# A two-layer recurrent kernel: TensorE's order in the second layer written out by hand, and half of a group's inverse moved into the next step

## The chip, the cores and the metric

The kernel runs on one core of a Trainium2 chip, as one launch. The metric is the device time of an execution in microseconds (us), lower being better. A core has five engines that run their own instruction streams in order and meet at semaphores: TensorE (PE: matmuls and transposes into PSUM; PEld is its weight load), VectorE (DVE), ScalarE (ACT), GpSimd (POOL), and SyncE (SP), which issues DMAs; POOL issues DMAs too.

## The reference

One sequence of 1024 tokens with 256 channels runs through two layers. Each layer normalises, computes an attention branch `s` and a mixture-of-experts branch `g` from the same normalised input, and adds `s * silu(g)`. The change is in the second layer. Its attention branch is a gated delta rule with 32 value heads and 16 key heads of 128 channels, behind a causal convolution of four taps; its expert branch picks 2 of 8 experts per token.

```python
    def step(S, xs):                       # per head, over the tokens
        qt, kt, vt, gt, bt = xs
        S = S * jnp.exp(gt)[..., None, None]
        kS = jnp.einsum('bhk,bhkv->bhv', kt, S)
        S = S + bt[..., None, None] * kt[..., :, None] * (vt - kS)[..., None, :]
        o = jnp.einsum('bhk,bhkv->bhv', qt, S)
        return (S, o)
    ...
    mixed = hidden_states @ W_qkv
    z = (hidden_states @ W_z).reshape(B, T, NV, DV)
    beta = jax.nn.sigmoid(hidden_states @ W_b)
    g = -jnp.exp(A_log) * jax.nn.softplus(hidden_states @ W_a + dt_bias)
    mixed = _silu(conv(mixed, conv_w))
    q, k, v = jnp.split(mixed, [key_dim, 2 * key_dim], axis=-1)
    q = _l2norm(q) * DK ** (-0.5)
    k = _l2norm(k)
    o = _gated_delta_rule(q, k, v, g, beta)
    o = o * jax.lax.rsqrt(mean(o * o) + 1e-06) * norm_w * _silu(z)
    return o.reshape(B, T, value_dim) @ W_out
    ...
x = x + s * g                              # g = silu(experts(xn))
```

## The kernel before

**The tiling.** The second layer works in `NG` = 8 groups of two key heads and four value heads. Time is cut into `NT` = 8 chunks of 128 tokens. Inside a chunk the delta rule is solved as matrices: a 128x128 triangular matrix per head and chunk (tile `m`) is inverted, and the state `S` is carried from chunk to chunk. Projections are done with a high and a low part of each operand, three matmuls of 128x512 for a product (`mm3`, L69 to L71).

**The streams.** Work is written as generators (streams), one letter each, and a string says in which order items are emitted:

- K, Q, V (`proj_k`, `proj_q`, `proj_v`): load weights (`load_w`, with `split_weights`: a DMA on SP's queue, one on POOL's, and a subtraction on POOL, L49), project into PSUM tile `pc`, and convolve (`conv_tile`: one ACT instruction and three DVE instructions of 128x511 for each half of 512 tokens, L678 and L681).
- P (`pre`): for each chunk the decay (`decay`: a POOL selection into `b`, L729, a matmul into `pe`, L731, an exponential into `d`), the scores of k with itself (`pkk`, L751) and the matrix `m` (L762). After the chunks comes the solve: POOL copies the 32x32 diagonal blocks into `Ad`, and 31 pairs of DVE instructions (L791, L793) with transposes around them (L785 to L800) give `X`, then `Un` and `Ut`. Then the inverse is completed on PE from 32x32 blocks (L818 to L827) and 64x64 blocks (L838, L843), in two halves of 16 matrices, each with POOL copies of `Ut` into `m` in front (L811).
- R (`recs`, `rec`): the recurrence, one item per chunk. `pkq` (L855) is the scores of q; then for both key heads `j`: four transposes into `pt` (L865), which ACT copies to `kd` and `bv`; `pk` (L883, L887), the state applied to k and q; DVE adds the first to `bv` (L885); `pw` (L893), the inverse applied to `bv`; ACT copies it to `W` (L895); `ps` (L900), whose result DVE adds to `S` (L909); and `pmw` (L915), which DVE adds to `v` (L918).
- O (`outp`, `out_half`): projection of z into `pz`, the gate in `gz` (L964 to L971, with transposes into `pto`, L970), a split into `yh` and `yl` (L973, on POOL), projection `pout` (L979 to L982), copies into `st`, and a DMA that adds to `sTd` in HBM (L988).
- F (`ffn_blocks`): blocks of 128 tokens of the experts, 12 at the start and 11 in the last step: transposes `pxt` (L1017), `pg` (L1024), transposes `pht` (L1033), `pd` (L1039), a store.
- U: the SiLU of what the convolutions left.

**What sets the order.** The scheduler orders all engines' instructions of the second layer from estimated times, dependencies and priorities. The strings `START`, `STEP` (for each group) and `LAST` (last group) only say in which order the items are emitted; P has a priority 3000 ahead, K one 1000 behind, and within `rec` the parts behind `pk` have 1000. `STEP` contains for one group the items of R of that group, O of the group before, and K, P, V, Q of the next. Instructions of the first layer already stand in an order written by hand (L519).

**PSUM.** Eight banks: ring C of three (`pc`, `pz`, `pto`, `pout` and F's), ring R of three (`pkq`, `pt`, `pk`, `pw`, `ps`, `pmw`) and ring B of two (`pe`, `pkk` and the inverse's `pm`, `pm2`, `pm3`). A tile takes the next bank of its ring, and its first matmul waits until the readers of the tile before in that bank are done.

**Before and behind the groups.** In front of `START` 16 indirect DMAs of POOL (`moe.scatter`, L215) put the tokens in the order of the experts. Behind the last group 16 indirect gathers (`moe.gather`, L222, into `yg`) bring the experts' results back, the sums in `sTd` are read into `sT`, transposed (`pfs`, L1190) and combined (L1191 to L1194).

```python
START = 'UPPPPPPPPPPPPVVVVQQUPPPPKKFFFFFFFFFFFFU'
STEP = 'OPPPPRPROPOPRPRVRPVOURPVRPRPPKKQPPRPQVU'
LAST = 'RROORRFFROOFFRFFRFFRFFR'
```

Of the kernel before, what the change touches and what calls it, by code (L numbers as in the profile page):

```python
# [8 lines left out]
F32 = mybir.dt.float32  # L9
# [15 lines left out]
def f32(ap):  # L25
    return ap.bitcast(F32)
# [93 lines left out]
class Blocks:  # L120
# [91 lines left out]
    def scatter(self, tc, t, x):  # L212

        for k in range(self.K):
            ins = self.nc.gpsimd.indirect_dma_start(out=self.xs[:, :], out_offset=bass.IndirectOffsetOnAxis(ap=self.to[:, t, k : k + 1], axis=0),  # L215
                                                    in_=x, in_offset=None).ins
            for other in self.scatters:
                tc.declare_no_dep(ins, other, reason="different rows")
            self.scatters.append(ins)

# [347 lines left out]
ZT = True  # L568
PBUFS = {'C': 3, 'R': 3, 'B': 2}
PS = {'pc': 'C', 'pxt': 'C', 'pg': 'C', 'pht': 'C', 'pe': 'B', 'pkk': 'B', 'pm': 'B', 'pm2': 'B', 'pm3': 'B', 'pkq': 'R', 'pt': 'R', 'pk': 'R', 'pw': 'R', 'ps': 'R', 'pmw': 'R', 'pz': 'C', 'pto': 'C', 'pout': 'C', 'pd': 'C', 'pfs': 'R'}  # L570
OLAG = 4
PRIO = {'P': 3000, 'U': 200, 'K': -1000}
AB = 'DVE'
RC = (0, 1000, 1000)
WINDOWS = True
FSEG = (12, 11)
NB = {'k0': 4, 'k1': 4, 'q0': 2, 'q1': 3, 'v': 8, 'm': 4, 'b': 3, 'd': 13, 'yh': 1, 'yl': 1, 'gz': 2, 'w': 3, 'S': 3, 'kd': 4, 'bv': 3, 'W': 1, 'bt': 1, 'tmp': 1, 'wr': 1, 'st': 1, 'ct': 1}
OR, KD, SP = 'Pool', 'ACT', True
GPRIO = 2000
EARLY = 'KK'  # L580
START = 'UPPPPPPPPPPPPVVVVQQUPPPPKKFFFFFFFFFFFFU'
STEP = 'OPPPPRPROPOPRPVRVPOURPVRPRPPKKQPPRPQVU'
LAST = 'RROORRFFROOFFRFFRFFRFFR'


def l1_block(ctx, tc, c, x1, wqkv, wz, wb, wa, convw, dtb, alog, normw, wout, wr, wg, wu, wd, out, x1_done=lambda: None):
# [27 lines left out]
    if ZT:  # L614
        nc.vector.tensor_scalar(nw, nw, 0.5, None, ALU.mult)
# [24 lines left out]
    silus = []  # L640

    def do_silus():
        while silus:
            d = silus.pop(0)
            table("silu", nc.scalar.activation(d, d, AF.Silu))

    def table(kind, ins):

        if not WINDOWS:
            return  # L650
        if kind != win[0]:
            win[0], win[1], win[2] = kind, win[2], []
        for before in win[1]:
            tc.add_manual_dep(ins.ins, before.name, mybir.DependencyInfo(mybir.DependencyClass.NoSync, mybir.DependencyReason.DATA),
                              reason="table sets")
        win[2].append(ins.ins)
# [11 lines left out]
    def conv_tile(w, j, n, dst):  # L668

        for h, d in enumerate(dst):  # L670
            p = ps("pc", [128, 512])
            project(p, w, j, slice(512 * h, 512 * h + 512))
            if h:

                nc.scalar.activation(d[:, 3:512], p[:, 3:512], AF.Copy, scale=cw[:, n, 3:4])
                nc.vector.scalar_tensor_tensor(d[:, 0:3], p[:, 0:3], cw[:, n, 3:4], last, ALU.mult, ALU.add)
            else:
                nc.scalar.activation(d, p, AF.Copy, scale=cw[:, n, 3:4])  # L678
            for i in (2, 1, 0):
                o = 3 - i  # L680
                nc.vector.scalar_tensor_tensor(d[:, o:512], p[:, 0 : 512 - o], cw[:, n, i : i + 1], d[:, o:512], ALU.mult, ALU.add)  # L681
            if not h:

                last = tiny.tile([128, 3], F32, tag="last", name="last")
                nc.vector.tensor_scalar(last, p[:, 509:512], cw[:, n, 0:1], None, ALU.mult)
                for i in (1, 2):
                    nc.vector.scalar_tensor_tensor(last[:, 0 : 3 - i], p[:, 509 + i : 512], cw[:, n, i : i + 1], last[:, 0 : 3 - i], ALU.mult, ALU.add)  # L687
        silus.extend(dst)
        if not WINDOWS:
            do_silus()  # L690
# [4 lines left out]
    def halves(pool, tag, b0, b1):  # L695
        return [pool.tile([128, 512], F32, tag=tag + str(h), name=tag, bufs=b) for h, b in enumerate((b0, b1))]

    def proj_k(g, G):

        G.k = []  # L700
        w = load_w(wqkv, slice(2048 + 256 * g, 2048 + 256 * g + 256))
        for j in range(2):
            G.k.append(halves(kp, "k", NB["k0"], NB["k1"]))
            conv_tile(w, j, 16 + 2 * g + j, G.k[j])
            yield
    def proj_q(g, G):
        G.q = []
        w = load_w(wqkv, slice(256 * g, 256 * g + 256))
        for j in range(2):
            G.q.append(halves(qp, "q", NB["q0"], NB["q1"]))  # L710
            conv_tile(w, j, 2 * g + j, G.q[j])
            yield

    def proj_v(g, G):

        G.v = []
        for j in range(2):
            w = load_w(wqkv, slice(4096 + 512 * g + 256 * j, 4096 + 512 * g + 256 * j + 256))
            G.v.append([vp.tile([128, 2, 512], F32, tag="v", name="v") for _ in range(2)])
            for i in range(2):  # L720
                conv_tile(w, i, 32 + 4 * g + 2 * j + i, [v[:, i, :] for v in G.v[j]])
                yield

    def decay(g, cc):

        p = ps("pe", [128, 512])
        for i in range(2):
            b = rc.tile([128, 4, 128], FR, tag="b", name="b", bufs=NB["b"])
            nc.gpsimd.affine_select(b, f32(gs)[:, cc, g, i, :, None].to_broadcast([128, 4, 128]), [[0, 4], [1, 128]], ALU.is_ge, 0.0,  # L729
                                    base=0, channel_multiplier=-1)  # L730
# [5 lines left out]
    def pre(g, G):  # L736
# [7 lines left out]
        rk = rc.tile([128, NT, 2], F32, tag="rk", name="rk")  # L744
        for cc in range(NT):
# [14 lines left out]
            if AB == "DVE":  # L760
                for u in range(4):
                    nc.vector.scalar_tensor_tensor(m4[:, u], p[:, u // 2, :], cf[:, cc, u : u + 1], d[:, u, :], ALU.mult, ALU.mult)  # L762
            elif AB == "Pool":
                for u in range(4):
                    nc.scalar.activation(m4[:, u], p[:, u // 2, :], AF.Copy, scale=cf[:, cc, u : u + 1])
                nc.gpsimd.tensor_tensor(m4, m4, d, ALU.mult)
            else:
                nc.vector.tensor_tensor(m4.rearrange("p (a b) t -> p a b t", b=2), p[:, :, None, :].to_broadcast([128, 2, 2, 128]), d.rearrange("p (a b) t -> p a b t", b=2), ALU.mult)
                nc.gpsimd.tensor_tensor(m4, m4, cf[:, cc, :, None].to_broadcast([128, 4, 128]), ALU.mult)

            nc.gpsimd.affine_select(d, d, [[0, 4], [1, 128]], ALU.is_ge, 0.0, base=0, channel_multiplier=-1)
            yield
        rsqrt(nc, tiny, rk.rearrange("p a b -> p (a b)"), kss.rearrange("p a b -> p (a b)"), 2 * NT)
# [14 lines left out]
        for j in range(31):  # L788
# [5 lines left out]
            if j % 8 == 7:  # L794
                yield
# [6 lines left out]
        pool_copy(nc, Un[32:64, :, 32:64], Un[32:64, :, 0:32])  # L802
        yield

        P = bt.tile([128, 32, 32], F32, tag="b2", name="P")
        for h in range(2):
            us = slice(16 * h, 16 * h + 16)
            M = G.m[h]
            for i in range(4):
                s = slice(32 * i, 32 * i + 32)  # L810
                pool_copy(nc, M[s, :, s], Ut[s, us])  # L811
            nc.gpsimd.memset(M[32:64, :, 0:32], 0.0)
            nc.gpsimd.memset(M[96:128, :, 64:96], 0.0)
            nc.gpsimd.memset(M[64:128, :, 0:64], 0.0)
            p = ps("pm", [128, 16, 32])
            for u in range(16):
                uu = 16 * h + u
                nc.tensor.matmul(p[32:64, u, :], M[0:32, u, 32:64], Un[0:32, uu, 0:32], start=True, stop=True, tile_position=(0, 32))  # L818
                nc.tensor.matmul(p[96:128, u, :], M[64:96, u, 96:128], Un[64:96, uu, 0:32], start=True, stop=True, tile_position=(64, 96))
            nc.scalar.copy(P[32:64, us, :], p[32:64])  # L820
            nc.scalar.copy(P[96:128, us, :], p[96:128])
            p = ps("pm", [128, 16, 32])
            for u in range(16):
                uu = 16 * h + u
                nc.tensor.matmul(p[0:32, u, :], P[32:64, uu, :], Ut[32:64, uu, :], start=True, stop=True, tile_position=(32, 0))
                nc.tensor.matmul(p[32:64, u, :], Ut[32:64, uu, :], P[32:64, uu, :], start=True, stop=True, tile_position=(32, 32))
                nc.tensor.matmul(p[64:96, u, :], P[96:128, uu, :], Ut[96:128, uu, :], start=True, stop=True, tile_position=(96, 64))  # L827
            nc.scalar.copy(M[0:32, :, 32:64], p[0:32])
            nc.scalar.copy(Un[32:64, us, 0:32], p[32:64])
            nc.scalar.copy(M[64:96, :, 96:128], p[64:96])  # L830
            yield
            for q in range(2):
                qs = slice(8 * q, 8 * q + 8)
                p = ps("pm2", [128, 8, 64])
                P2 = P[64:128, us].rearrange("p (a b) c -> p a (b c)", b=2)
                for u in range(8):
                    uu = 8 * q + u
                    nc.tensor.matmul(p[64:128, u, :], M[0:64, uu, 64:128], Un[0:64, 16 * h + uu, :], start=True, stop=True, tile_position=(0, 64))  # L838
                nc.scalar.copy(P2, p[64:128])
                p = ps("pm3", [64, 8, 64])  # L840
                for u in range(8):
                    uu = 8 * q + u
# [401 lines left out]
```

## Time and profile before

| What | Value |
|---|---|
| Median of three executions | 1928.91 us (1925.61 to 1929.60) |
| The profiled execution | 1922.61 us, span 1920.6 us |
| Mean clock granted to TensorE in it | 0.918 |
| PE busy | 1581.3 us (82%), 11566 matmuls |
| DVE busy | 1339.8 us (70%) |
| ACT busy | 1053.3 us (55%) |
| POOL busy | 754.5 us (39%) |
| DMA | 147.28 MB, mean 77 GB/s |

The profile is one execution. "Busy" is the time in which an engine executes; the matmuls are pipelined, so their busy time is longer than the distance between two starts. Its second part cuts the span into 40 slices of 48 us, with a digit for the busy share in tenths. Costly groups of instructions are listed with the idle time of their engine in front of them and what released it:

```profile
L69 PE MATMUL pc<-xnh,wl 128*128 128x512 f32 x256 | 118.5, 464 | 42.1 <-DVE last L687 12.3
L893 PE MATMUL pw<-bv,m 128*128 128x128 f32 x512 | 92.4, 300 | 71.5 <-DVE bv L885 67.6
L681 DVE SCALAR_TENSOR_TENSOR v<-pc,cw,v 128x511 f32<-128x511 f32 (+2 forms) x192 | 140.3, 740 | 2.6 <-ACT v L678 1.7
L907 POOL TENSOR_TENSOR S<-S,eC 128x256 f32<-128x256 f32 x96 | 59.6, 621 | 182.9 <-PE pk L887 147.8
```

In the second line, for example, the 512 `pw` matmul passes were busy for 92.4 us at 300 ns each, and PE stood idle for 71.5 us in front of them, 67.6 of it until DVE had written `bv`.

### The profile page before, as it was taken

The page shows a single profiled execution, that of the slowest core. Times are in us where ns is not written, and L with a number is a line of the kernel's source. Part 1 is how long each engine was busy: PE and PEld are TensorE (multiplying, and loading weights), DVE is VectorE, ACT ScalarE, POOL GpSimd, SP SyncE. Part 2 cuts the span into 40 slices and gives each one's busy share as a digit, 9 for nine tenths or more (in the row PEclk, how much of TensorE's full clock was granted, in tenths as well). Part 3 has the DMA queues.
Part 4 walks back from the last instruction along what each step waited for, and adds up shares of the span by engine and source line. Part 5 has one row for each costly group of instructions (what it writes and reads, how often), then busy time and mean ns, then how long its engine had stood idle before and what let it go on. Part 6 is the DMA issues. An engine that isn't in the chain of part 4 may idle for free. (4 is left out here: it accounts for less than half of the span.)

```text
span 1920.6 us, 34083 instructions
## 1 busy us (share of the span) xinstructions
PE 1581.3 (82%) x11566; PEld 1207.1 (63%) x11566; DVE 1339.8 (70%) x3833; ACT 1053.3 (55%) x2844; POOL 754.5 (39%) x949
## 2 busy tenths in 40 slices
PE   4789988989656699889799799799799799879854
PEld 3446666666444377667677577677677677658643
DVE  6675565555659827947977978978978977963332
ACT  2345545544423356646677566576576566646632
POOL 4051000000616425157347347347347347433263
PEclk9799999999858679979999999999999999989977
DMA  8024444441362421012103203103103103204535
GB/s 261 12 86 129 127 120 126 131 133 60 104 147 78 116 69 52 17 35 61 39 24 67 44 24 72 39 24 72 39 24 72 39 23 72 63 16 98 139 88 124
DMA packets 149755, 147.28 MB, mean 77 GB/s; under 512 B 22013, under 2 KB 137037, under 8 KB 149581
## 3 DMA queue, kind: packets, MB, share of 16 engines
q1 hardware_dynamic: 115853, 97.15, 17.1%
q0 software_dynamic: 33728, 47.96, 11.9%
q8 instruction: 92, 1.51, 0.3%
q14 instruction: 82, 0.67, 0.1%
HBM read 91.59 MB, written 49.28 MB: 73 GB/s over the span
## 5 line engine op out<-in xcount | busy, mean ns | idle before, releaser
L493 ACT ACTIVATE pe<-p 128x1024 f32<-128x1024 f32 (+1 forms) x192 | 154.6, 813 | 113.6 <-PE p L491 83.5
L427 DVE CUSTOM_DVE_ANT_0 junk<-p,maskm 128x128 bf16<-128x128 f32 (+3 forms) x256 | 125.2, 489 | 59.7 <-PE p L421 48.9
L69 PE MATMUL pc<-xnh,wl 128*128 128x512 f32 x256 | 118.5, 464 | 42.1 <-DVE last L687 12.3
L893 PE MATMUL pw<-bv,m 128*128 128x128 f32 x512 | 92.4, 300 | 71.5 <-DVE bv L885 67.6
L681 DVE SCALAR_TENSOR_TENSOR v<-pc,cw,v 128x511 f32<-128x511 f32 (+2 forms) x192 | 140.3, 740 | 2.6 <-ACT v L678 1.7
L893 PEld LDWEIGHTS pw<-bv,m 128*128 128x128 f32 x512 | 74.8, 194 | 100.2 <-DVE bv L885 87.0
L421 PE MATMUL p<-kz,qT 128*128 128x512 f32 (+3 forms) x384 | 116.7, 396 | 19.7 <-DMA kz<-kT 11.5
L907 POOL TENSOR_TENSOR S<-S,eC 128x256 f32<-128x256 f32 x96 | 59.6, 621 | 182.9 <-PE pk L887 147.8
L487 PE MATMUL p<-q,kz 128*128 128x512 f32 (+3 forms) x384 | 122.6, 404 | 6.8 <-ACT pe L493 2.2
L923 ACT ACTIVATE sq<-v 128x128 bf16<-128x128 f32 x256 | 77.3, 307 | 88.8 <-DVE v L918 78.7
L49 POOL TENSOR_TENSOR wl<-wr,wh 128x512 fp32r<-128x512 f32 x68 | 88.4, 1301 | 94.5 <-DMA wh<-in_L_attn_W_z_dram 24.2
L895 ACT ACTIVATE W<-pw,cf 128x128 f32<-128x128 f32 x256 | 79.9, 365 | 60.0 <-PE pw L893 58.4
L965 DVE SCALAR_TENSOR_TENSOR gz<-gz,pz 128x512 f32<-128x512 f32 x64 | 43.8, 685 | 92.6 <-ACT gz L964 92.4
L71 PE MATMUL pc<-xnl,wh 128*128 128x512 f32 x256 | 107.4, 420 | 0.0
L70 PE MATMUL pc<-xnh,wh 128*128 128x512 f32 x256 | 107.2, 419 | 0.0
L874 ACT ACTIVATE kd<-pt,eR 128x128 f32<-128x128 f32 x256 | 79.8, 361 | 45.7 <-PE pt L865 44.3
L423 DVE TENSOR_REDUCE mx<-p 128x2 f32<-128x1024 f32 x64 | 77.8, 1223 | 32.7 <-PE p L421 32.1
L793 DVE TENSOR_TENSOR X<-X,Ad 128x31 f32<-128x31 f32 (+15 forms) x248 | 97.6, 394 | 3.8
L791 DVE TENSOR_TENSOR Ad<-Ab,X 128x31 f32<-128x31 f32 (+15 forms) x248 | 93.4, 376 | 3.3
L421 PEld LDWEIGHTS p<-kz,qT 128*128 128x128 f32 x384 | 66.1, 202 | 40.8 <-ACT pe L493 10.1
L973 POOL TENSOR_TENSOR yl<-gz,yh 128x512 fp32r<-128x512 f32 x64 | 84.0, 1315 | 19.3 <-ACT yh L972 19.1
L69 PEld LDWEIGHTS pc<-xnh,wl 128*128 128x128 f32 x256 | 51.9, 203 | 62.3 <-DVE last L687 12.8
(356 smaller groups left out, 5062.8 us busy)
## 6 DMA issues: line engine op xcount, KB each, us to landing
sTd<-st POOLq DMA_DIRECT2D x32, 512.0 KB, 6.4
gw<-_L_ffn_gate_up_proj_dram SPq DMA_DIRECT2D x64, 192.0 KB
l0xs<-zero SPq DMA_DIRECT2D x1, 8320.0 KB
xb<-l0xs SPq DMA_DIRECT2D x32, 256.0 KB
l0ys<-y SPq DMA_DIRECT2D x32, 256.0 KB
wh<-in_L_attn_W_qkv_dram POOLq DMA_DIRECT2D x32, 256.0 KB, 3.1
wr<-in_L_attn_W_qkv_dram SPq DMA_DIRECT2D x32, 256.0 KB
dw<-in_L_ffn_down_proj_dram SPq DMA_DIRECT2D x64, 96.0 KB
```

The costliest lines, as they stand in the source:

```text
L49: nc.gpsimd.tensor_tensor(lo, raw, f32(hi), ALU.subtract)
L69: nc.tensor.matmul(out, al, bh, start=start, stop=False)
L70: nc.tensor.matmul(out, ah, bh, start=False, stop=False)
L71: nc.tensor.matmul(out, ah, bl, start=False, stop=stop)
L421: nc.tensor.matmul(p[:, h - h0, :n], qT[:, 128 * i : 128 * i + 128], kz[:, h, 512 * j : 512 * j + n], start=True, stop=True)
L427: nc.vector.tensor_tensor_reduce(junk[:, :n], p[:, h - h0, :n], maskm[:, o : o + n], 1.0, -3e38, ALU.add, ALU.max, accum_out=mx[:, i, h, 0:1])
L487: nc.tensor.matmul(p[:, h - h0, :n], kz[:, h, 128 * kt : 128 * kt + 128], q2[:, 512 * qb + o : 512 * qb + 512], start=True, stop=not diag)
L493: nc.scalar.activation(e[:, :, :n], p[:, :, :n], AF.Exp, scale=SC)
L681: nc.vector.scalar_tensor_tensor(d[:, o:512], p[:, 0 : 512 - o], cw[:, n, i : i + 1], d[:, o:512], ALU.mult, ALU.add)
L791: nc.vector.tensor_tensor(t, Ab[:, j, j + 1 : 32, None].to_broadcast([128, n, m]), X[:, j, None, 0:m].to_broadcast([128, n, m]), ALU.mult)
L793: nc.vector.tensor_tensor(X[:, j + 1 : 32, 0:m], X[:, j + 1 : 32, 0:m], t, ALU.add)
L893: nc.tensor.matmul(pw[:, 0, i, :], M[:, 4 * (cc % 4) + 2 * j + i, :], bv[:, i, :], start=True, stop=True)
```

## The change

Nothing is computed differently. The streams are cut into smaller items, their emission is spread by position instead of by a string, and PE executes the second layer's instructions in the order of emission. The other engines are still ordered by the scheduler.

- `weave` takes entries (stream, number of items, from, to), spreads that many items evenly between two positions in the step, sorts, and emits. `START`, `STEP` and `LAST` are lists of such entries; all runs within `tc.manual_schedule` for PE.
- `rec` becomes five kinds of items: `scores` (`pkq`), `turn` (transposes), `state` (`pk` and the add to `bv`), `delta` (`pw`, and the copy, now in place into `bv`), and `update` (`ps`, `S`, `pmw`, squares). Per chunk both `j` are interleaved, 9 items, and `scores` and `turn` of the next chunk come early. The recurrence has 72 items a group instead of 8. `ps` uses the second half of the bank of `pw`. `bv` has 4 buffers instead of 3; `W` is gone.
- P is split into P (decay and scores, 8 items), X (the solve, 32 items) and I (inverse, 12 items). In `STEP` six items of I (a half, for chunks 0 to 3) come late in the step in which X was solved, and the other six (chunks 4 to 7) early in the next step.
- K, Q and V give one item per half tile. The last half of Q of a group is projected in the next step (`late_q`), with its weights loaded a second time.
- O: a half is cut in two items for `pz` and `gz`, two for `pto` and `yh`, `yl`, and two for `pout`; `pout` of one half (`pend`) comes after `pz` of the next. Weights are loaded one item ahead.
- F: a block is cut into `turn_x`, `up`, `turn_h` and `down`, and the blocks overlap: `turn_h` and `down` of a block come between `turn_x` and `up` of the next. Its work tile is an `m` buffer of its own instead of `gz`, `yh` and `yl`. All 12 first blocks are in `START`, ahead of the recurrence of group 0; the last two blocks of the other 11 come at the end of `LAST`.
- The scatters are emitted within `START` and ordered on POOL behind the last decay selection emitted before them.

```diff
-START = 'UPPPPPPPPPPPPVVVVQQUPPPPKKFFFFFFFFFFFFU'
-STEP = 'OPPPPRPROPOPRPRVRPVOURPVRPRPPKKQPPRPQVU'
-LAST = 'RROORRFFROOFFRFFRFFRFFR'
+START = (("P", 8, 0, 0.3), ("S", 8, 0.3, 0.31), ("V", 9, 0, 0.45), ("Q", 5, 0.15, 0.5), ("U", 1, 0.52, 0.52), ("X", 32, 0.3, 0.6), ("I", 6, 0.7, 1),
+         ("F", 52, 0.35, 1), ("K", 1, 0.9, 0.9))
+STEP = (("R", 72, 0, 1), ("K", 5, 0, 0.08), ("U", 1, 0.09, 0.09), ("O", 24, 0, 0.45), ("P", 8, 0.09, 0.38), ("X", 32, 0.37, 0.5),
+        ("V", 1, 0.27, 0.27), ("V", 4, 0.36, 0.58), ("Q", 1, 0.45, 0.45), ("V", 4, 0.62, 0.82), ("Q", 3, 0.52, 0.7), ("U", 1, 0.85, 0.85),
+        ("I", 6, 0.02, 0.36), ("I", 6, 0.66, 0.9), ("K", 1, 0.92, 0.92), ("O", 1, 0.93, 0.93))
+LAST = (("R", 72, 0, 1), ("I", 6, 0.02, 0.36), ("K", 1, 0, 0.1), ("U", 1, 0.12, 0.12), ("O", 24, 0, 0.45), ("O", 1, 0.5, 0.5), ("O", 12, 0.55, 1),
+        ("F", 48, 0.3, 1.2), ("O", 12, 1, 1.4))
...
+    def late_q(g, G):
+        if G.q[1][1] is None:
+            w = load_w(wqkv, slice(256 * g, 256 * g + 256))
+            G.q[1][1] = half(qp, "q", 1)
+            conv_half(w, 1, 2 * g + 1, 1, G.q[1][1])
...
+        def delta(cc, j):
+            kd, bv = st[cc, j]
+            pw = st[cc, j, 0] = ps("pw", [128, 2, 2, 128])
+            for i in range(2):
+                nc.tensor.matmul(pw[:, 0, i, :], G.m[cc // 4][:, 4 * (cc % 4) + 2 * j + i, :], bv[:, i, :], start=True, stop=True)
+            with tc.high_priority(offset=RPRIO):
                 for i in range(2):
+                    nc.scalar.activation(bv[:, i, :], pw[:, 0, i, :], AF.Copy, scale=G.cf[:, cc, 2 * j + i : 2 * j + i + 1])
+
+        def update(cc, j):
...
+            kd, W = st.pop((cc, j))
+            pS = st.pop((cc, j, 0))[:, 1]
...
+        scores(0)
+        yield
+        turn(0, 0)
+        yield
+        turn(0, 1)
+        yield
+        for cc in range(NT):
+            more = cc + 1 < NT
+            for j in range(2):
+                state(cc, j)
+                yield
+            if more:
+                scores(cc + 1)
+                yield
+            for j in range(2):
+                delta(cc, j)
+                yield
+            if more:
+                turn(cc + 1, 0)
+                yield
+            for j in range(2):
+                update(cc, j)
+                yield
+            if more:
+                turn(cc + 1, 1)
+                yield
...
+    def weave(*lists):
+        items = []
+        for s, n, a, b in lists:
+            items += [(a + (b - a) * (i + 0.5) / n, s) for i in range(n)]
+        for _, s in sorted(items, key=lambda x: x[0]):
+            next(streams[s], None)
...
-    for t in range(NT):
-        xt = rc.tile([128, D], F32, tag="kd", name="xt", bufs=NB["kd"])
-        nc.sync.dma_start(xt, xnd[128 * t : 128 * t + 128, :])
-        moe.scatter(tc, t, xt)
-    run(START)
-    for g in range(NG):
-        run(LAST if g == NG - 1 else STEP if g else STEP.replace("O", "", OLAG))
-    run("FFFF" + "".join(s * 16 for s in "PROF"))
+    def scatters():
+        for t in range(NT):
+            xt = rc.tile([128, D], F32, tag="kd", name="xt", bufs=NB["kd"])
+            nc.sync.dma_start(xt, xnd[128 * t : 128 * t + 128, :])
+            for ins in moe.scatter(tc, t, xt):
+                order_only(ins, last_b[0].ins)
+            yield
+
+    streams["S"] = scatters()
+    with tc.manual_schedule(engines={mybir.EngineType.PE}):
+        weave(*START)
+        for g in range(NG):
+            weave(*(LAST if g == NG - 1 else [x for x in STEP if g or x[0] != "O" or x[1] == 1]))
```

## The prediction

> **What bounds the kernel now.** I read the slices of the whole span first, then windows of one step of the second layer, then the waits in that step, and the chain that ended last. The first layer (to about 530 us) is not touched.
>
> ```profile
> PE   4789988989656699889799799799799799879854
> DVE  6675565555659827947977978978978977963332
> PEclk9799999999858679979999999999999999989977
> ```
>
> From slice 17 on the pattern 7-9-9 for PE repeats every three slices of 48 us: one step is 144 us. The last `pmw` matmul (L915) of groups 0 to 7 stands at 812, 981, 1118, 1263, 1406, 1550, 1698 and 1837 us in the trace, so six steps (812 to 1698) take 886, 147.7 each, and the last group 139. The slices at clock 5 to 7 (520 to 720 us) are the start of the layer; those behind 1837 are its tail of 83 us.
>
> ```profile
> 672.00:720.00 48.00, 45.55 (x563) 35.97 (x562) 14.23 (x39) 24.90 (x66) 11.35 (x18) 0.72 0.24 69
> 1296.00:1344.00 48.00, 43.95 (x266) 36.92 (x264) 38.83 (x126) 33.00 (x93) 37.13 (x51) 1.00 0.37 72
> 1344.00:1392.00 48.00, 38.23 (x201) 29.27 (x200) 47.07 (x119) 28.00 (x102) 17.84 (x23) 0.96 0.17 39
> 1392.00:1440.00 48.00, 43.68 (x598) 35.62 (x599) 35.83 (x90) 34.94 (x100) 21.87 (x25) 1.00 0.09 24
> ```
>
> The columns are the stretch, its length, busy PE, PE loads, DVE, ACT and POOL, the clock, the DMA share and GB/s. In the middle third DVE is busy 47.07 of 48 us: there the solve (L785 to L800, 53 us from first to last instruction) is a chain on DVE. In the others PE is the fuller engine, 43.7 to 44.0, but not full. So a step is a DVE phase of 53 us and a PE phase of 91 us, one behind the other, since the inverse needs the solve and the next solve needs the next scores.
>
> ```profile
> PE pw L893 <- DVE bv L885: 9.1, 6, 2.4
> PE pc L69 <- DVE k L681: 2.1, 1, 2.1
> PE pk L883 <- DVE v L918: 1.6, 1, 1.6
> DVE gz L965 <- ACT gz L964: 10.1, 4, 3.4
> DVE gz L971 <- PE pto L970: 3.9, 1, 3.9
> DVE S L911 <- PE ps L900: 2.5, 1, 2.5
> ```
>
> These are waits between 1344 and 1488 us: total, times, longest. PE's 18 us of gaps (144 less the 125.9 of the last three windows) are half recurrence (`pk`, then DVE, then `pw` with nothing put between). A third loss shows as instructions: two kinds of inverse matmul are interleaved, and a pair of L843 with a pair of L818 takes 0.43 us (1421.59 to 1422.02), though 32 alone take 0.7 us and eight of 64x64 0.9. I put that at 4 to 5 us a step.
>
> **The floor of a step.** Start to start, a 128x512 matmul takes 0.23 us (1418.83 to 1419.06), a pass of an fp32 128x128 0.112 (two passes each), of a 128x256 0.218, of a 64x64 0.058. A step has 208 of the first (96 `pc`, 48 `pz`, 48 `pout`, 16 `pe`): 48.3 us. 124 fp32 128x128 matmuls (`pkq`, `pkk`, `pw`, `ps`, `pmw`): 27.8. 28 `pk`: 12.2. 96 transposes: 10.8. The inverse: 9. Sum 108, in both kernels: the edit removes no matmul. DVE's instructions of a step, each at its duration less 83 ns (what successive starts show), sum to 115 in both.
>
> **The change, part by part.**
>
> *Steady step.* In the new order PE issues 53.5 us of its 108 before the last decay and score matmuls (`pe`, `pkk`) that the solve needs, 31.8 more while the solve runs, and then stands at the first 32x32 matmul of the inverse, in order, until the solve's X, its transposes and the POOL copies are there. Behind it stand the recurrence, three or four projections and the rest: 23 us. So the cycle is solve + latency + (23 + 53.5) us of PE. The solve is 46.9 us of DVE instructions after, 49.7 before (52.9 measured, x1.064): 50. PE's 76.5 at its old ratio in the PE phase (90.7 measured for 73.4, x1.24) would be 95; without the interleaving (4.5 us) and without the `pw` waits (two thirds of 9.1: another stream's item now lies between) the ratio is 1.10: 84. Bounds x1.04 to 1.17: 80 to 90. Latency from the solve's last transpose to the first matmul: four POOL copies of 0.61 us and some memsets, behind whatever POOL has begun (up to 1.3 us): 6 taken, bounds 3 to 8. Together 140, bounds 133 to 148. PE waits some 21 us there (50 + 6 - 31.8 x 1.10), hidden as long as DVE is on X. Six steps: 6 x 140 = 840 for 886: **-46**.
>
> *PSUM.* `ps` now shares `pw`'s bank, which is held from delta to update: two of three banks of the ring R. `pmw`, the next transposes and `pk` then take the third in turn, and each waits for its last reader on DVE or ACT. Price of one: a 0.33 us read behind at most one 0.74 us convolution. Sixteen updates a step; the trace has only four waits of the kind (`pk` on `v`, 5.0 us in the whole run). I take 0.2 us each, inside the ratio 1.10; high end 0.75, which is the slower rival.
>
> *Late Q half.* Seven extra weight loads: two queues' DMAs each and one POOL subtraction of 1.30 us. POOL is busy 77 of 144 us: nothing; without this cover 9 us in all. `W` in place of `bv` frees no time (same copy).
>
> *Start.* F's blocks (12, some 10 us each from 631 to 749) ran beside group 0, whose last `pmw` stood at 812. Now they are in PE's order ahead of all of group 0's recurrence. The indirect scatters are held behind the decay's POOL work (about 612), so the first F transpose stays near 641. A block is 2.5 us of PE at full clock, 4 at the 0.64 to 0.72 shown; skewed by halves I take 5 to 6: start ends at 700 to 715, and group 0 (no output projection, 104 us of DVE issue x1.06 = 110) ends at 810 to 825; bounds 800 to 845, since its first chunk may wait for the last block. I take 820: **+8**. F's work tile takes one of the four `m` buffers in place of `gz`, `yh` and `yl`; group 1's `m` needs it only after F's end: nothing, and at worst one block, 6 us. SP's queue gets F's loads (192 and 96 KB) an item ahead of their use, at a DMA share of 0.24 to 0.41 in these windows: nothing, at worst the 1.4 us that PE waited for `fin` once in the last group.
>
> *Last group.* Before: 38.6 us for the first chunk (half of it the inverse, which now lies in the step before) and 101 for seven. Largest of PE and DVE issue, chunk by chunk, sums to 108.6 after; x1.08 = 117, bounds 110 to 127: **-22**.
>
> *Tail.* The chain that ended last:
>
> ```profile
> 1871.05 1.30 POOL yl L973
> 1872.35 1.24 POOL wl L49
> ...
> 1876.42 6.11 DMA sTd<-st
> 1882.55 3.99 DMA sT<-sTd
> ...
> 1894.26 6.46 DMA sTd<-st
> ...
> 1902.20 6.42 DMA sTd<-st
> 1908.63 3.58 DMA sT<-sTd
> ```
>
> Four additions to sTd and two reads stay. What can go is PE waiting on POOL (L982 for `yl` 10.0 us, L979 for `wl` 7.5): 16 gathers of 1.27 us stood in POOL's queue ahead of `yl` and `wl`. Now eight of them come behind. Weights of the output projection are loaded an item ahead. 83 us become 72, bounds 64 to 82: **-11**.
>
> Against the profiled execution (1922.61, span 1920.6, so 2 us around it): 1922.6 + 8 - 46 - 22 - 11 = 1852. The median of the runs shown is 1928.9, 6 more; I forecast 1856, on its own bounds 1820 to 1895.
>
> **A rule against it.** The windows give clock 0.54 for 528 to 576 us, 0.72 for 672 to 720, 0.96 to 1.00 in a steady step, and 128x512 matmuls 0.43 us apart where it is low, 0.23 where it is full. My sum keeps the steady clock, because waits in it (longest 2.4 us) left it there.
>
> The Trainium skill, page "TensorE: Matmul & The Clock Gate", section "What's actually happening", says that the array falls to half its clock after an idle window of about 3.4 us and needs a busy one of that length to return. By that rule the in-order wait of some 21 us at the inverse is followed by 3.4 us at half speed, which as an estimate from the page adds 1.7 us a step, 12 in all: 1868 instead of 1856. The trace of before has no such wait in a steady step.
>
> **Rivals.**
> - *The DVE phase decides alone.* The solve keeps its 53 us, and the wait moves from `pw` to the inverse with all else behind it: 95 + 53 = 148, nothing won in six steps. Start, last group and tail remain: 1922.6 + 8 - 22 - 11 + 6 = 1904. For it: DVE 47.07 of 48. Against: PE's other gaps are real.
> - *Low bounds meet.* Steps of 134 (-82), last group 112 (-27), tail 70 (-13), start even: 1807. For it: floors of 108 and 115 lie far below 144. Against: the solve chain has no slack.
> - *Slower: the ring R.* PE can no longer step around a bank that is not free: each of 16 updates a step waits 0.75 us, 12 us a group. Steps 152 (+26), last group 129 (-10), start +20, tail -11: 1922.6 + 25 + 6 = 1954. It decides from about 9 us a group (71 us saved over eight groups), 0.55 us an update. For it: DVE is 70 to 98% busy, so a bank's reader seldom starts at once; before, the ring turned over freely. Against: high priority is given to these reads.
> - *No net effect*: between the two, gains of the end eaten by the ring: 1925 to 1933.
>
> **How the numbers follow.** Forecast 0.45, solve alone 0.20, low bounds 0.13, slower 0.18, no effect 0.04. About 0.2% is what a measurement of this kernel can tell from no change. Forecast, solve alone and low bounds are faster: 0.78; same 0.04; slower 0.18. The range 1790 to 1935 takes in nearly all of the first three and the edge of the slower one.
>
> **What would show it.** Group ends (last `pmw`) near 820, then every 140; PE's longest wait in a step at the first 32x32 matmul, on POOL or DVE, near 20 us; no `pw` waits on `bv` above 1 us; last group 117; tail 72 with PE not waiting on `yl`. Wrong would be: `pmw`, `pt` or `pk` waiting on DVE's `S` or `v` by over 9 us a step (the ring); F blocks still 10 us apart; a steady clock under 0.95.

## The result, and the profile after

The changed kernel takes 2029.5 us (median of 4, 2027.6 to 2034.5), the kernel before 1929.3 (median of 4) measured beside it: a ratio of 1.052 (95% interval 1.049 to 1.055), 100 us slower where 73 less were forecast. The profiled execution has a span of 2025.8 us, 105 over before, at a mean clock of 0.886 (before 0.918).

The slices of the span after, 51 us each:

```profile
PE   4789889988464884896777678579678867859993
DVE  6665556554597579569658757856965875785442
PEclk8799999998666997999898888799888878989996
```

PE's 9 in two slices of three has become 7 and 8, with a 5 or 6 in every step, and its clock falls to 7 and 8 there. No engine is fuller than before: PE's busy time is 1549 us (1581 before), DVE's 1343 (1340). The time is waiting.

The last `pmw` of each group (L959 after) says where it lies:

| Part | Before | Forecast | After |
|---|---|---|---|
| End of group 0 | 812.2 | 820 | 837.9 |
| Six steps, sum (each) | 885.3 (147.6) | 840 (140) | 1006.2 (167.7) |
| Last group | 139.8 | 117 | 122.5 |
| Tail to the end of the span | 83.3 | 72 | 59.2 |

Last group and tail came as forecast or better (-17 and -24 us). Group 0 lost 26 and the steps lost 121. One step in four windows (the columns as in the prediction: busy PE, PE loads, DVE, ACT, POOL, the clock, DMA):

```profile
1341.00:1387.00 46.00, 35.36 (x345) 29.17 (x344) 29.35 (x84) 27.02 (x73) 25.04 (x29) 0.93 0.22 47
1387.00:1427.00 40.00, 33.97 (x225) 28.80 (x223) 27.41 (x95) 24.81 (x73) 30.50 (x43) 0.96 0.28 54
1427.00:1476.00 49.00, 27.94 (x141) 23.25 (x141) 47.08 (x121) 22.45 (x70) 14.78 (x17) 0.82 0.20 43
1476.00:1508.00 32.00, 30.21 (x352) 26.11 (x353) 16.98 (x38) 21.99 (x74) 9.15 (x13) 0.90 0.07 18
```

The third window is the solve: DVE is full (47 of 49 us), as before, but PE does only 28 us there. PE's waits in that step (total, times, longest), which answer to those of before:

```profile
PE pm L849 <- DVE Un L822: 16.0, 1, 16.0
PE pc L69 <- POOL wl L49: 7.6, 1, 7.6
PE pout L1065 <- POOL yl L1051: 3.3, 1, 3.3
PE pmw L959 <- DVE S L953: 3.2, 3, 2.0
PE pout L1062 <- ACT yh L1050: 1.7, 1, 1.7
PE pmw L959 <- ACT sq L911: 1.4, 2, 1.0
```

The 9.1 us of `pw` waiting for `bv` are gone. In their place PE stands 16.0 us at the first 32x32 matmul of the inverse, 7.6 for the late Q half's weights, and 1 to 3 us each at eight others, the four longest of which are shown. Over the run the first is 122.6 us in 7 waits, the second 44.1 in 6. The second is on the chain of waits that ended last (start, length, what), here its POOL part:

```profile
1350.45 6.53 POOL v L1033 x7
...
1357.44 1.04 POOL v L1033
1358.48 0.68 POOL wh L48
```

All eight normalisations of `v` become ready together and go first in POOL's queue; the DMA of the late weights is issued behind them, at 1358.5, and PE, which wanted the weights at 1355.4, has them at 1363.

From the trace, a step can be measured as a closed cycle: the solve (first transpose `Ab` to last transpose `Ut`), PE from `Ut` to the last score matmul `pkk` of the next group, and the way from there to the next `Ab` (DVE writes `m`, POOL copies `Ad`). The cycle that begins with the solve of group 4, in us, each part from the start of its first instruction to the start of the next part's:

| Kernel | Solve | `Ut` to last `pkk` | `pkk` to `Ab` | Cycle |
|---|---|---|---|---|
| Before | 51.0 | 78.9 | 13.5 | 143.4 |
| After | 51.6 | 102.2 | 15.5 | 169.3 |
| without the second load | 50.3 | 94.4 | 15.8 | 160.5 |
| half the solve | 34.5 | 104.7 | 14.1 | 153.3 |
| 14 `d` buffers | 51.3 | 105.3 | 11.4 | 168.2 |
| inverse later | 59.1 | 88.8 | 15.4 | 163.3 |
| `ps` in its own tile | 48.3 | 102.6 | 13.3 | 164.2 |
| three costs out, by hand | 57.7 | 81.4 | 13.3 | 152.3 |
| no order by hand | 56.8 | 81.7 | 12.6 | 151.1 |
| Q whole, own tile, no order by hand | 59.6 | 77.1 | 12.4 | 149.1 |

So the loss is in the second column: 102 us for 79. PE's matmuls between those two points are 77.7 us of issue after and 66.8 before; the rest is lost time, 24 us for 12. A cycle differs from the next by a few us: over the six cycles from group 1 on, the three parts average 49.4, 103.4 and 14.8 us after, and 55.8, 79.3 and 12.7 before, where the first solve takes 75.

### The profile page after: what moved, and what is told of

Read it like the earlier page. It is cut to its first block, busy times and chain, and to the rows that moved or that the text cites. A ratio compares the mean times of both kernels' runs of the same rounds, so it can differ in the third digit from the quotient of the medians.

```text
span 2025.8 us, 34085 instructions
## 1 busy us (share of the span) xinstructions
PE 1549.0 (76%) x11566; PEld 1219.7 (60%) x11566; DVE 1342.7 (66%) x3833; ACT 1062.0 (52%) x2844; POOL 771.1 (38%) x963
## 4 chain that ended last, share of the span: by engine, by line
PE 33%; DVE 19%; POOL 6%; ACT 5%; issue 3%; DMA 2%; SPq 0%; POOLq 0%; DVEq 0%; ACTq 0%
DVE X L817 3%; DVE Ad L815 3%; PE pmw L959 2%; POOL v L1033 2%; DVE v L686 2%; PE pk L923 2%; DVE q L686 2%; PE pk L924 2%; PE pc L69 2%; PE pc L70 2%; PE pc L71 2%; PE pm L870 2%; PE pt L904 2%; PE pw L936 2%; PE pw L948 1%
## 5 line engine op out<-in xcount | busy, mean ns | idle before, releaser
L69 PE MATMUL pc<-xnh,wl 128*128 128x512 f32 x256 | 125.9, 492 | 58.3 <-POOL wl L49 44.1
L428 DVE CUSTOM_DVE_ANT_0 junk<-p,maskm 128x128 bf16<-128x128 f32 (+3 forms) x256 | 125.3, 489 | 60.4 <-PE p L422 49.4
L49 POOL TENSOR_TENSOR wl<-wr,wh 128x512 fp32r<-128x512 f32 x75 | 98.5, 1314 | 118.2 <-DMA wh<-in_L_attn_W_out_dram 36.9
L849 PE MATMUL pm<-Un,m 32*32 32x32 f32 x512 | 24.8, 214 | 122.6 <-DVE Un L822 122.6
L1033 POOL TENSOR_TENSOR v<-v,rs 128x512 f32<-128x512 f32 x64 | 64.4, 1042 | 128.1 <-DVE rs L63 124.7
L952 POOL TENSOR_TENSOR S<-S,eC 128x256 f32<-128x256 f32 x96 | 66.7, 694 | 118.2 <-DVE S L953 66.9
L959 PE MATMUL pmw<-bv,d 128*128 128x128 f32 x512 | 84.5, 290 | 34.9 <-DVE S L953 19.1
L929 ACT ACTIVATE v<-pk,eG 128x128 f32<-128x128 f32 x224 | 71.1, 369 | 66.1 <-DVE bv L927 61.6
L849 PEld LDWEIGHTS pm<-Un,m 32*32 32x32 f32 x512 | 22.9, 129 | 127.3 <-DVE Un L822 125.5
L959 PEld LDWEIGHTS pmw<-bv,d 128*128 128x128 f32 x512 | 68.7, 194 | 44.6 <-DVE S L953 22.9
L927 DVE SCALAR_TENSOR_TENSOR bv<-pk,eG,bv 128x128 f32<-128x128 f32 x224 | 67.7, 344 | 38.2 <-PE pk L924 36.3
```

The costliest lines, as they stand in the source:

```text
L69: nc.tensor.matmul(out, al, bh, start=start, stop=False)
L428: nc.vector.tensor_tensor_reduce(junk[:, :n], p[:, h - h0, :n], maskm[:, o : o + n], 1.0, -3e38, ALU.add, ALU.max, accum_out=mx[:, i, h, 0:1])
L959: nc.tensor.matmul(pm[:, i, :], G.d[cc][:, 2 * j + i, :], W[:, i, :], start=True, stop=True)
L1033: nc.gpsimd.tensor_tensor(o, o, rs[:, i, :, None].to_broadcast([128, 4, 128]), ALU.mult)
```

## Experiments

Some kernels were measured where the kernel before takes 1970 to 1978 us; the first layer, which no kernel here changes, is some 40 us longer there. So totals are compared as ratios to the kernel before measured beside them, and steps (mean of the six between the ends of groups 0 and 6) directly: the same steps took 152.9 us in run 6, where the kernel before takes 1975, and 152.8 in run 9, where it takes 1926.

**1. Without the second load of weights.**

```diff
-            w = load_w(wqkv, slice(256 * g, 256 * g + 256))
+            w = w or load_w(wqkv, slice(256 * g, 256 * g + 256))
...
-            late_q(g - 1, Gs[g - 1])
+            late_q(g - 1, Gs[g - 1], w)
```

> Leaves out the seven second weight loads of the late Q half: that half is projected with the K weights that are still there, so seven loads (14 DMAs, seven POOL subtractions) are not done and the last half of Q of each group has other values. Theory: a step of the changed kernel is one cycle (last score matmul to solve 15.5 us, solve 50, PE from the inverse to the next last score 102), and the wait of PE for the late weights (L49, six times 7.6 us, 44 in all) lies in its PE part: steps of 160 for 167.7, about 1985 us. Rival (the wait is slack: PE would stand that much longer at the inverse, 20 us a step there): about 2028.

Steps of 159.6, ratio 1.020 (1.011 to 1.030). The wait on `wl` is gone and nothing took its place: 8 us a step, as the cycle said. PE still waits 121.7 us at the inverse, so this cost was not slack.

**2. Priority for P and X on the other engines.**

```diff
+            if s in 'PX':
+                with tc.high_priority(offset=3000):
+                    next(streams[s], None)
```

> P and X get the priority 3000 that P had before; PE's order stays, only DVE, ACT and POOL are ordered anew. Theory of the cycle: the 15.5 us from the last score matmul to the solve's first transpose, 6 to 7 of them because the instructions for m (L789) stand on DVE behind a square root and behind recurrence steps that wait for PE, shrink to about 9: 7 steps x 6.5 = 45, about 1985 us. Rival (ring R of PSUM and PE's in-order waits set the step): 2025 to 2035.

Steps of 168.0, ratio 1.045 (1.038 to 1.052): no effect on the steps, and the way from `pkk` to the solve stays at 15.7 us. The way is not made of a poor choice among ready instructions; run 5 shows what it waits for.

**3. The inverse later.**

```diff
-        ("I", 6, 0.02, 0.36), ("I", 6, 0.66, 0.9), ("K", 1, 0.92, 0.92), ("O", 1, 0.93, 0.93))
+        ("I", 6, 0.02, 0.36), ("I", 6, 0.84, 1), ("K", 1, 0.92, 0.92), ("O", 1, 0.93, 0.93))
```

> The six items of the inverse in a step go from 0.66-0.90 to 0.84-1.00, so some 15 us of PE's other work stands before the wait for the solve (16 to 24 us a step, 122.6 in all). Theory of the cycle: that work leaves the PE part of the cycle (15 us at the ratio 1.3 is 20), steps of 148, about 1905 to 1930 us. Rival (ring R and the many small in-order waits set PE's pace, the wait at the inverse is only where the slack is taken): 2010 to 2030.

Steps of 164.5, ratio 1.037 (1.034 to 1.040): 3 us a step for the 20 expected. The wait at the inverse falls (71.5 us in all for 122.6) and PE's part of the cycle from 102 to 89, but the solve grows from 51 to 59: what PE now does during the solve gives DVE convolutions and sums, which stand between the solve's instructions. In the solve of group 4, DVE is busy 57.6 of 59 us, 48.3 of 51 in the changed kernel; the durations of its instructions that are not the solve's sum to 39 us there for 27, the convolutions of `v` alone to 15.5 for 8.8. More than half of what left PE's part (7.5 of 13.4 us) came back in DVE's.

**4. `ps` in a tile of its own.**

```diff
-            pS = st.pop((cc, j, 0))[:, 1]
+            st.pop((cc, j, 0))
             if cc + 1 < NT:
+                pS = ps("ps", [128, 2, 128])
```

> ps gets a tile of its own in ring R again, as before, instead of the second half of the bank of pw. Rival of the prediction (ring R): the waits of pmw and pt for S, v and squares, some 7 us a step, go: 1975 us or less. Theory of the cycle: most of these waits lie outside its PE part or are filled by the next one: 2010 to 2030.

Steps of 163.5, last group 118.9, ratio 1.032 (1.029 to 1.036). The shared bank costs 4 us a step. The slower rival of the prediction (ring R) was the right kind of cost at a third of its size, 4 for 12, and no more than a sixth of the 28 by which the forecast of a step was off.

**5. One more buffer for `d`.**

```diff
-'b': 3, 'd': 13
+'b': 2, 'd': 14
```

> 14 buffers for d instead of 13 (b has 2 instead of 3 to make room). The last decay of a step then waits for the buffer of chunk 1 of the recurrence instead of chunk 2. Theory (the recurrence lies in the cycle through d): the exponential of the last decay, which stands on ACT until the last pmw of chunk 2, comes as soon as its matmul is done; 15.5 us from the last score matmul to the solve become about 9, steps of 161 to 163. Rival (DVE's order and its waits for PE hold m back, d is not the last to come): steps of 166 to 168 as in the changed kernel.

Steps of 166.5, ratio 1.046 (1.038 to 1.054). The way from `pkk` to the solve did shrink, from 15.5 to 11.4 us (14.8 to 11.1 over six cycles), so the buffer that the recurrence frees was what the last decay waited for. But the step gained only 1: over six cycles the solve grew by 1.7 (49.4 to 51.1) and PE's part by 0.7 (103.4 to 104.1; the 105.3 of the table is a long one). The mechanism was right, and most of the gain was given back.

**6. No order by hand at all.**

```diff
-    with tc.manual_schedule(engines={mybir.EngineType.PE}):
+    with ExitStack():
         weave(*START)
```

> All of the change except the order by hand: the scheduler orders PE too, from the new streams. Theory (what costs is that PE stands in a fixed order behind the solve and the late weights): PE goes on with other work there, steps of 145 to 152, and the time within 1 to 2% of the kernel before. Rival (the finer items, the shared bank or the split inverse cost it): steps stay at 160 or more, 4% or more over the kernel before.

Ratio 0.9998 (0.998 to 1.002): as long as the kernel before. Steps of 152.9, last group 142.1, tail 58.6. The order by hand alone costs 15 of the 20 us a step by which the change is slower; the tail's gain does not need it. Its PE waits in one step:

```profile
PE pm L849 <- DVE Un L822: 9.9, 1, 9.9
PE pto L1048 <- POOL v L1033: 6.0, 1, 6.0
PE pk L923 <- DVE v L962: 2.1, 2, 1.3
```

PE waits for the solve here too, but 9.9 us for 16.0; over the run this wait falls from 122.6 to 41.6 us, and the one for the late weights comes 3 times (30.5 us) instead of 6 (44.1).

**7 and 8. Three parts together, and with 14 buffers of `d`.** The edits of runs 3 and 4, and

```diff
+            if late_load:
+                order_only(ins.ins, late_load[j].ins)
```

behind the normalisation of `v`, where `late_load` holds the late half's DMA and its subtraction.

> Three parts together: the six inverse items at 0.84-1.00, ps in a tile of its own, and POOL's late weights ordered in front of the second half of the normalisations of v. Alone the first two took 4 us a step each; the loads left out took 8, the order may keep 4 of them. If these parts are separate: steps of 154 to 157. If they share one cause (slack moved between waits): 160 or more.

> The three parts and 14 buffers of d: if d lies in the cycle, 4 to 7 us a step less than the three parts alone; otherwise the same.

Steps of 161.2 and 161.8, ratios 1.024 (1.016 to 1.032) and 1.025 (1.016 to 1.034). PE still waits 6.4 us for the late weights in a step, since two subtractions for `yl` stand ahead of them on POOL in place of the four normalisations: the attempt to save the load failed, the 6.5 us a step that were won are no more than those of runs 3 and 4, and 14 buffers add nothing.

**9. The order by hand in the last group only.**

```diff
-    with tc.manual_schedule(engines={mybir.EngineType.PE}):
-        weave(*START)
-        for g in range(NG):
-            weave(*(LAST if g == NG - 1 else [x for x in STEP if g or x[0] != "O" or x[1] == 1]))
+    weave(*START)
+    for g in range(NG - 1):
+        weave(*[x for x in STEP if g or x[0] != "O" or x[1] == 1])
+    with tc.manual_schedule(engines={mybir.EngineType.PE}):
+        weave(*LAST)
```

> The order by hand only for PE's last group (LAST); the start and the steps are ordered by the scheduler from the new streams, as in the run without any order by hand, which took as long as the kernel before, with steps of 153 and a last group of 142 us. Theory (the hand order loses in the steps, where PE stands behind the solve and the late weights, and wins in the last group, where there is no solve: 122 for 142): 20 us less than the kernel before, ratio 0.990. Rival (the last group's gain belongs to the half of the inverse and the state left by a hand-ordered step, not to its own order): ratio 1.00.

Ratio 1.007 (1.005 to 1.009), last group 157.1 us: my theory fell and the rival held. The scheduler leaves the inverse of the last group to its beginning, where the hand order then stands 15.4 us behind the solve. All 448 inverse matmuls of that group come behind the end of group 6 here, 224 in the changed kernel. So the 17 us that the change won in the last group belong to work that its longer steps had done beforehand, as the rival had it.

**10. The same with `ps` in its own tile.**

> The same, with ps in a tile of its own in ring R. If the shared bank also costs the scheduler's order 4 us a step: 24 to 30 us less, ratio 0.975 to 0.98. If the scheduler steps around a held bank: 0.990 as without it.

Ratio 0.9996 (0.998 to 1.001), steps of 151.1, 2 less than without. The scheduler steps around a held bank in part.

**11. Half of the solve.**

```diff
+            if j % 2 == 0:
                 nc.vector.tensor_tensor(t, ...)
                 nc.vector.tensor_tensor(X[:, j + 1 : 32, 0:m], X[:, j + 1 : 32, 0:m], t, ALU.add)
```

> The changed kernel, leaving out every second of the 31 pairs of DVE instructions of the solve (15 pairs, some 24 of its 49 us; X has other values). Theory (solve, PE part and decay chain are one cycle): PE's wait of 16 to 24 us at the inverse goes nearly to nothing and the step falls by that: 146 to 152 us, total ratio to before 0.98 to 1.00. Rival (PE's pace over all its small waits sets the step, the wait at the inverse is slack): steps of 162 or more, ratio 1.03 or more.

Steps of 152.4, ratio 0.997 (0.995 to 0.999). The waits of one step no longer name the inverse:

```profile
PE pc L69 <- POOL wl L49: 8.8, 1, 8.8
PE pout L1066 <- POOL yl L1052: 3.5, 1, 3.5
PE pmw L960 <- DVE S L954: 2.6, 2, 2.0
```

The solve shrank by 17 us, the step by 15, and the other two parts of the cycle stayed within 2.5 us (104.7 and 14.1). Solve, PE's part and the way back are one cycle, and the wait at the inverse is a part of it, not slack. The price in the expectation was too high: the solve's own instructions are busy for 28.6 of the 51.6 us in the changed kernel and for 16.6 here, 12 us less and not 24; the rest of the solve is other streams' work on DVE, of which less stands in a shorter solve (18 us for 24).

**12. The three costs taken out under the order by hand** (the edits of runs 1, 3 and 4).

> The changed kernel with ps in its own tile, the six inverse items at 0.84-1.00, and without the seven second weight loads (the last half of Q of each group is projected with K's weights and has other values). If the three costs add (4, 4 and 8 us a step): steps of 152, ratio 1.005. If one takes the place of the other: 157 or more, ratio 1.02 or more.

Steps of 154.2, ratio 1.004 (1.001 to 1.006): 13.5 us a step for 8, 4 and 3 alone. They add, nearly.

**13 to 15. All of Q in its own step**, with room made by one buffer of `b`:

```diff
-'q0': 2, 'q1': 3,
+'q0': 2, 'q1': 4,
...
-            for h in range(2 - (g > 0 and j)):
+            for h in range(2):
...
-("Q", 3, 0.52, 0.7)
+("Q", 4, 0.52, 0.75)
```

> The changed kernel with all of Q projected in its own step (no second load; the second half of q has 4 buffers for 3, b has 2 for 3 to make room). If the cost of the late half is its load (POOL's subtraction comes 7.6 us after PE wants it): 7 to 8 us a step less, 160, ratio 1.02 to 1.03, as when only the loads were left out. Rival (the work of that half costs as much in the solve's stretch of the step, where DVE is full): 164 or more, ratio 1.035 or more.

Steps of 158.0, ratio 1.017 (1.013 to 1.022): 10 us a step, 2 more than the load alone. Most of what the late half costs is its load.

With the edits of runs 3 and 4:

> The same with ps in a tile of its own and the six inverse items at 0.84-1.00, order by hand as in the changed kernel. If the parts add as they did with the loads left out (steps of 154, 1.0038): 152 to 156, ratio 1.00 to 1.01. A hand order that stands behind the solve does not get under the steps of before (147.7).

Ratio 1.004 (1.001 to 1.006), steps of 155.1. A hand order without the three costs still has steps 7.5 us over those of before, and 10 over its last four (144.9, where these are 155.3).

Without any order by hand, and with the edit of run 4:

> The new streams without any order by hand, all of Q in its own step, ps in a tile of its own. Theory (the 5 us by which the scheduler's steps of the new streams, 153, exceed those of before, 147.7, are the shared bank and the late load): steps of 146 to 149, and with the shorter tail (59 us for 83) ratio 0.975 to 0.985, faster than both kernels. Rival (the finer items cost it): steps of 150 to 153, ratio 0.99 to 1.00.

Ratio 0.983 (0.979 to 0.987), 1940.8 us where the kernel before takes 1970: faster than both kernels. Steps of 148.9 (the last four 146.9; before 147.6 and 144.9), last group 137.8, tail 59.0. Its waits in one step:

```profile
PE pto L1049 <- POOL v L1034: 7.1, 1, 7.1
PE pz L69 <- DVE gz L1050: 5.0, 2, 3.7
PE pk L923 <- DVE v L963: 2.5, 1, 2.5
```

The inverse does not appear among the longest of them. So 4 of the 5 us by which the scheduler's steps exceeded those of before were the shared bank and the late half, 1 to 2 us remain, and the finer items cost no more than that. Most of what the new streams gain is the tail, 59 us for 83; which of their parts shortens it was not tested.

## Why the prediction was wrong

- **The step that failed: "the ratio is 1.10: 84"**, and with it "together 140". PE's 76.5 us of issue (77.7 in the trace) took 102, a ratio of 1.31, over the 1.17 that I took as the upper bound. (The same stretch of the old trace, without the way back that my 1.24 held, is 78.9 us for 66.8, 1.18.) The way back of 15.5 us comes on top: 118 us where the sum has 84 and 6. With the solve, 51.6 for 50, this is the measured cycle of 169 for 140. I let the two old losses go to nothing, and they did (no wait for `bv` is left in the step, and the 64x64 inverse matmuls come in blocks of 0.92 us); but all that I put in their place was the ring's 0.2 us an update. PE runs in a fixed order in both kernels, and mine has it stand longer at late operands than the scheduler's order of the same streams (at the inverse 16.0 us for 9.9, run 6). Runs 1, 4 and 6 give the size: 8 us for the late load, 4 for the bank, and 15 for the order by hand, which holds a part of both.
- **"Late Q half ... nothing; without this cover 9 us in all" was wrong by its measure.** I compared POOL's busy time over the step with one subtraction's length. What counts is when the subtraction is reached: eight normalisations of 1.04 us stand in front. 44 us of waiting in the run, 48 by run 1 (8 a step).
- **The latency was put in the wrong place.** "6 taken" was from the solve's last transpose to the first inverse matmul: measured 0.1 us (PE waits for `Un` alone), in the trace of before too (1404.30 to 1404.36). The long way is from the last score matmul to the solve, 15.5 us, and the trace of before showed it at 13.5; I had not measured it as a term of its own.
- **"PE waits some 21 us there, hidden as long as DVE is on X"**: the wait came as forecast (16 to 24 us), and the cycle that the sum was built on, solve and PE one behind the other, is right: run 11 took 17 us from the solve and 15 from the step. But it is no room that can be filled freely (run 3), because PE's other work feeds the DVE queue in which the solve stands.
- **The solve kept its length** (50 us forecast, 49 to 54 measured from first to last instruction). It is not a chain of 50 us, though: in the solve of group 4 before, too, its own instructions are busy for only 28.7 of 51.0 us, with other streams' work between. The rival in which DVE decides alone (148 us a step) failed by its 95 us of PE, like the forecast.
- **Start**: F's blocks came 5 us apart (forecast 5 to 6) and ended at 704 (700 to 715). Group 0 then took 134 us for 110: it too waits at the inverse, 23.7 us. **Last group** 122.5 for 117: the size right, but its reason only half (run 9). **Tail** 59 for 72: PE's wait for `wl` is gone, 7.9 us on `yl` remain.
- **The ring as a rival**: its price was taken as 12 us a group, and 4 was measured. It gave a time of 1954 and so was nearest to the result, for a reason that explains a sixth of it. Of the three signs against the forecast that I had named, one appeared: a clock under 0.95 in three of the step's four windows (0.82 to 0.96). `pmw` and `pt` waited 4.5 us in the step for `S` and `v`, not over 9, and F's blocks were no longer 10 us apart.
- **The clock.** In the changed kernel the clock stays at half after the wait at the inverse. In pieces of 3 us from the wait's end (the clock is the figure behind the five busy times):

```profile
1476.00:1479.00 3.00, 2.89 (x67) 2.65 (x68) 1.83 (x2) 0.85 (x2) 2.08 (x3) 0.50 0.00 0
1479.00:1482.00 3.00, 3.00 (x9) 2.34 (x8) 0.61 (x2) 0.93 (x3) 2.74 (x6) 0.50 0.00 0
1482.00:1485.00 3.00, 3.00 (x111) 2.80 (x110) 1.76 (x4) 1.78 (x4) 1.08 (x2) 0.98 0.02 5
```

The six projections at 1479.5 start 0.43 us apart (0.79 between the first two), against 0.23 elsewhere. My sum had kept the steady clock, and even the trace of before did not (0.96 in the window of the solve). The rule of the Trainium skill ("TensorE: Matmul & The Clock Gate", section "What's actually happening") was right in kind: an idle window of that length drops the clock to half. The page's window of about 3.4 us is also that of the trace, whose stretches at half clock last 3.4 us or a multiple of it; but the 3.4 us at half speed that I took behind the wait are 6 here, so by an estimate from the trace some 3 us are lost at the inverse, and 1.5 more behind the 7.6 us wait for the late weights (0.50 from 1363 to 1366). The same step has two more stretches at half clock, outside PE's part of the cycle (they are shown at the end). An estimate for the PE parts of six steps, the issue time of all matmuls that start at half clock, is 6.3 us a step after and 2.6 before. None of this was tested by itself, and run 11, without the wait at the inverse, did not have a shorter PE part (104.7 for 102.2).

What stays open: the runs separate the late load, the bank and the place of the inverse, together 13.5 of the 28 us by which a step was off. Without these costs the hand order (155.1) still stands 6 us over the scheduler's (148.9); its waits of 1 to 4 us for `yl`, `yh` and others were not taken apart.

## What to carry to other kernels

Before an order is fixed by hand on one engine, list for every item in it when its operands come from the other engines' queues, and count each late one: in a fixed order all that stands behind it waits too, and a scheduler's order that looks untidy may be the one that hides it. Where a step is a cycle over several engines, measure its parts in the old trace as separate terms, the short latencies too, and ask of a moved item whether it goes into the cycle or out of it. A load is not hidden because its engine is half idle: look at what stands in that queue when the load is wanted.

## What the runs showed of the hardware

In the trace of the changed kernel every change of the granted clock lies on one grid of 3.41 us. In the six steps the clock fell to half 29 times, for 3.4, 6.8, 17.1 or 20.5 us (128x512 matmuls then start 427 ns apart, else 230). By the profile's busy times, in the 3.41 us before each fall PE had been busy for 2.4 us or less, and every stretch of the grid at the full clock with less than 1.5 us was followed by one at half; in the last stretch before each return it had been busy for 2.8 us or more. Short waits are enough for that. Here it is one of 2.0 us (until 1416.0), and two of 1.7 and 3.3 us (until 1424.1 and 1428.3):

```profile
1413.88:1417.29 3.41, 1.38 (x11) 1.23 (x11) 3.13 (x12) 0.99 (x5) 2.49 (x3) 1.00 0.49 96
1417.29:1420.70 3.41, 3.41 (x13) 2.93 (x12) 1.11 (x4) 1.99 (x6) 1.27 (x1) 0.50 0.80 133
1424.10:1427.50 3.40, 0.94 (x3) 0.46 (x3) 2.03 (x6) 2.10 (x4) 3.17 (x6) 1.00 0.00 0
1427.50:1434.30 6.80, 6.01 (x14) 4.81 (x15) 6.35 (x20) 1.84 (x5) 3.40 (x5) 0.50 0.00 0
```

So the length of a wait does not tell what it costs behind its end: the half clock lasted 4.5 to 7.5 us behind the seven waits of 16 to 24 us, 2.8 to 3.9 behind the five of 7.6, and 6.1 behind the one of 3.3. At half the clock about half of such a stretch is lost where PE is never idle in it, 2 to 4 us behind a wait at the inverse, as an estimate.
